# Attention weights of six chunks made in layer 0 for all queries, and a second tile set moved into the attention's pools

## Chip, cores and metric

The kernel runs on one core of one Trainium2 chip. The metric is the device time of one execution in microseconds (us). Three runs of the kernel before took 10067.42 us in the median, 10067.21 to 10070.63.

## What is computed

Two layers over 3,327 nodes of 128 features, with a dense 0/1 adjacency matrix `adj`. Cut to what matters:

```
# layer 0
h = relu(layernorm(x))
agg = adj.T @ h / deg                      # deg: row sums of adj, 0 taken as 1
x = x + relu(batchnorm(agg @ W_n.T + b_n + h @ W_c.T + b_c))
# layer 1: attention with 128 batches d, n = 3327 queries and keys, 8 features each
h = relu(layernorm(x))
q, k, v = (h @ W.T reshaped to (128, n, 8) for W in Wq, Wk, Wv)
a = softmax(q @ k.T / sqrt(128) + adj + adj, axis=keys)
x = x + (a @ v).reshape(n, 1024) @ Wo.T
```

The same `2 * adj` is added to the scores of all 128 batches. So exp(score + 2 adj) = exp(score) * exp(2 adj), and the second factor, called the weight here, can be made once.

## The kernel before

**Layer 0.** The 3,328 padded rows are 26 chunks of 128. For each chunk c, SyncE (SP) loads 128 rows of `adj` (1.66 MB) into one of three buffers `a`; TensorE (PE) adds their product with the normalised features into seven PSUM banks (`gather`, L500), ScalarE (ACT) sums the rows for the degree (L507, written to `junk`), and VectorE (DVE) takes their maximum (L510). A buffer is loaded again when all three have read it. Beside each chunk one small step of `beside` runs through the eighth bank, `aside`: a transpose and ACT's copy (L412), a product with W_c and ACT's copy (L421), or, for chunks 15 to 18, a square of a weight matrix on GpSimd (POOL, L428), a product and a maximum on DVE. From chunk 19 on, `spread` puts 1/deg into diagonal tiles on POOL (L442), PE spreads them (L446) and ACT copies (L450). After the loop come the batch norm, the second layer norm, and the projections of q, k and v for the first 416 rows, which are stored to `qT`, `kT` and `v1` in HBM (the k parts on SP's queue, the q parts on ACT's, v on POOL's). POOL's queue stores `hd` and `xd` at the end.

**Attention.** 32 groups of four batches (index i), each with 7 blocks of up to 480 queries (y) and 13 steps (s): 2,912 steps. The 26 key chunks are cut in two kinds. Of the 18 "plain" ones, DVE adds the adjacency to the scores (L923, tile `at` from `adjT`) and ACT takes the exponential (L968). For the other 8 (from chunk `WC` = 18 on), ACT takes the exponential of the scores alone (L932) and POOL multiplies by the weight (L935, tile `wt` from `wd` in HBM). PE makes the scores (L783) and the products with v (L668). Steps are written out by hand in program order, engine by engine; `fetch` issues loads of `at` and `wt` two steps ahead on SP.

**Weights.** `wd` holds 8 x 128 x 3,328 weights. Those of the first 512 queries are made after layer 0's loop, in two halves of 256 queries (`weigh_early`, L539 and L540). Those of block y + 1 are made in block y of group 0 by `more_weights`: every third step it stores the last two chunks (L804), loads two chunks (L812, 480 KB), and two steps later ACT takes their exponential (L817, tile `t`). Both use `low`, 0 or -1e30, as the bias.

**Sets.** `sets` has two sets of q, k, v tiles, one for even and one for odd groups. Both lie in a pool that is open for the whole kernel, as does `ks`, in which k is loaded before POOL sorts it (L192). `first_loads` (L877 to L892) borrows set 1's k to load the first group's k, 8 DMAs, and 16 DMAs follow for q. `loads` fetches the next set while a group runs: in group 0 from step 39 on, in later groups from step 4.

```
more_weights(i, y, s)
if x > 1:
    for args in others[:2]:
        nc.sync.dma_start(*args)
    del others[:2]
due = len(waiting) == LAG
```

Of the kernel before, what the change touches and what calls it, by code (L numbers as in the profile page):

```python
# [9 lines left out]
F32 = mybir.dt.float32  # L10
F32R = mybir.dt.float32r
I32 = mybir.dt.int32
AF = mybir.ActivationFunctionType
ALU = mybir.AluOpType
AX = mybir.AxisListType
PSUM = bass.MemoryType.PSUM
# [5 lines left out]
P = 128  # L22
NC = 26
T = N * D
NP = NC * P
NB = 512
# [4 lines left out]
SAFE = 30.0  # L31
SU = NC // 2
WC = 18
CH = 4 * NP // D
NG = D // G
DOUBLE = (3, 7, 11)
PARTS = (3, 7, 8)

# [8 lines left out]
def tile_two_layer_gnn(  # L47
# [17 lines left out]
    nc = tc.nc  # L65
# [57 lines left out]
    FROM = [3 * SU] + [LAG + 1] * (NG - 1)  # L123

    qkp = ctx.enter_context(tc.tile_pool(name="qk", bufs=1))
    ksp = ctx.enter_context(tc.tile_pool(name="ks", bufs=1))

    def tile_set(x):
        q = qkp.tile([P, NP], F32R, name=f"q{x}")
        k = qkp.tile([P, NC, P], F32R, name=f"k{x}")  # L130
        v = qkp.tile([P, G, NC, H + 1], F32, name=f"v{x}")

        nc.vector.memset(v[96:, :, NC - 1, :], 0.0)
        return q, k, v

    sets = [tile_set(x) for x in range(2)]

    def q_loads(q, p0, d, n0=0, n=NP):

# [22 lines left out]
            vd[:, (P - 1) * W :].rearrange("b (o w) -> o b w", o=1),  # L162
        )]

    def loads(tiles, d):

        q, k, v = tiles

        def dma(*args):
            return lambda: nc.sync.dma_start(*args)  # L170

        def batch(b):
            return d + b if b else d

        qs = [dma(*a) for b in range(G) for a in q_loads(q, 32 * b, batch(b))]
        vv = [dma(*a) for a in v_loads(v, d)]
        todo = []
        for half in range(2):

            ks = ksp.tile([P, NP // 2], F32R, name="ks")  # L180
            for b in range(G):
                todo += [
                    dma(*a)
                    for a in k_loads(ks, 32 * b, batch(b), half * (NP // 2), NP // 2)
                ]
            todo += vv if half == 0 else []
            todo += [qs.pop(0) for _ in range(2) if qs]
            for c in range(0, NC, 4):
                n = min(4, NC - c)

                def sort(ks=ks, c=c, n=n, half=half):
                    nc.gpsimd.tensor_copy(  # L192
                        k[:, c : c + n, half * 64 : half * 64 + 64],
                        ks.bitcast(F32).rearrange("g (p c) -> g c p", c=NC)[:, c : c + n, :],
                    )

                todo.append(sort)
                if qs:
                    todo.append(qs.pop(0))
        assert not qs  # L200
        return todo
# [105 lines left out]
    with tc.tile_pool(name="l0", bufs=1) as l0, tc.tile_pool(  # L307
        name="l0adj", bufs=3
    ) as ap, tc.tile_pool(name="l0s", bufs=4) as sp, tc.tile_pool(
        name="l0last", bufs=1  # L310
    ) as ll, tc.tile_pool(name="l0p", bufs=1, space=PSUM) as pp:


        xs = ll.tile([P, NC, D], F32, name="xs")
# [21 lines left out]
        tiles = []  # L336

        def load(c):

            a = ap.tile([P, 7 * NB], F32, name="a")  # L340
            nc.sync.dma_start(a[:, :N], adj[c * P : (c + 1) * P, :])
            tiles.append(a)
            if c in (1, 2):
                c0, c1 = (4, 14) if c == 1 else (14, NC - 1)
                nc.sync.dma_start(xs[:, c0:c1, :], xr[:, c0:c1, :])
            if c == 2:
                for p0, p1 in pieces(N - (NC - 1) * P):
                    nc.sync.dma_start(
                        xs[p0:p1, NC - 1, :], x[(NC - 1) * P + p0 : (NC - 1) * P + p1, :]
                    )  # L350
            if c in (5, 7, 9):
                i = (c - 5) // 2
                nc.sync.dma_start(wqk[i], (WqT, WkT, WvT)[i])
            if c == 11:
                nc.sync.dma_start(wo, WoT.rearrange("(e p) o -> p e o", p=P))
# [114 lines left out]
        def set_flag():  # L470
# [12 lines left out]
            nc.vector.tensor_copy(low_half, aside[:, :2])  # L483
            yield

        load(0)
        for c in range(NC):
            a = tiles[c]
            if c + 1 < NC:
                load(c + 1)  # L490
            if c < NQ:
                if c == 0:
                    stats(c)
                normalise(c, A)
                if c + 1 < NQ:
                    stats(c + 1)

            def gather(i0, i1):
                for i, (n0, w) in list(enumerate(blocks))[i0:i1]:
                    nc.tensor.matmul(  # L500
                        acc[i][:, :w], A[:, c, :], a[:, n0 : n0 + w],
                        start=(c == 0), stop=(c == NC - 1),
                    )

            last = c == NC - 1
            gather(0, 4 if last else len(blocks))
            nc.scalar.activation(  # L507
                junk, a[:, :N], AF.Copy, accum_out=deg[:, c : c + 1]
            )
            nc.vector.tensor_reduce(  # L510
                amax[:, c : c + 1], a[:, :N], AX.X, ALU.max, apply_absolute_value=True
            )
            if last:
                nc.vector.tensor_reduce(top, amax, AX.X, ALU.max)
                flags = set_flag()
                next(flags)
                gather(4, len(blocks))
                next(flags)
                spreading = spread(NQ - 1)
                next(spreading)  # L520
            if c >= 1:
                beside(c - 1)
            if c - 1 == 2 * NQ + 4:
                set_bound()

            i = c - 2 * NQ - 5
            if 0 <= i < NQ - 1 and 4 * i + 4 <= c:
                for _ in spread(i):
                    pass
        weights = []  # L530
        for n0 in range(0, NB, NB // 2):
            a = ap.tile([P, 7 * NB], F32, name="a")
            a8 = a[:, : 8 * (NB // 2)].rearrange("p (c n) -> p c n", c=8)
            nc.sync.dma_start(a8, adjr[:, WC:, n0 : n0 + NB // 2])
            weights.append((a8, n0, NB // 2))

        def weigh_early():
            a8, n0, w = weights.pop(0)
            nc.scalar.activation(a8, a8, AF.Exp, bias=low, scale=2.0)  # L539
            nc.sync.dma_start(wd[:, :, n0 : n0 + w].rearrange("c p n -> p c n"), a8)  # L540

        bst = l0.tile([P, NQ, 6], F32, name="bn_st")
        bmv = l0.tile([P, 2], F32, name="bn_mv")
# [11 lines left out]
        for i, (n0, w) in enumerate(blocks):  # L555
            s = slice(n0, n0 + w)
            nc.vector.tensor_tensor(B2[:, s], acc[i][:, :w], B2[:, s], ALU.mult)
            nc.tensor.matmul(acc[i][:, :w], wn, B2[:, s], start=True, stop=True)
            if i >= 1:
                hidden(i - 1)  # L560
            if i == 0:
                next(spreading)
            if i in (0, 1):
                weigh_early()
        hidden(NQ - 1)
        nc.vector.bn_aggr(bmv, bst.rearrange("p i s -> p (i s)"))
# [140 lines left out]
    def attention():  # L707
# [3 lines left out]
        with tc.tile_pool(name="exd", bufs=4) as ep, tc.tile_pool(  # L711
            name="adj", bufs=4
        ) as ap, tc.tile_pool(name="adw", bufs=3) as wp, tc.tile_pool(
            name="exf", bufs=6
        ) as fp, tc.tile_pool(name="res", bufs=2) as rp, tc.tile_pool(
            name="wk", bufs=2
        ) as wk, tc.tile_pool(name="psc", bufs=3, space=PSUM) as psc, tc.tile_pool(
            name="pav", bufs=1, space=PSUM
        ) as pav:


            avs2 = [pav.tile([P, NB], F32, name=f"av{x}") for x in range(2)]
            for av in avs2:
                nc.vector.memset(av, 0.0)
            if True:
# [5 lines left out]
                def at(i):  # L731
                    return i * G
# [62 lines left out]

                def more_weights(i, y, s):

                    k, phase = divmod(s, 3)
                    if i or y + 1 >= len(qblocks):
                        return  # L800
                    n0, w = qblocks[y + 1]
                    c = WC + 2 * k
                    if phase == 0 and k:
                        nc.sync.dma_start(  # L804
                            wd[c - 2 - WC : c - WC, :, n0 : n0 + w].rearrange("c p n -> p c n"),
                            have["w"][:, :, :w],
                        )
                    if c == NC:
                        return
                    if phase == 0:  # L810
                        have["w"] = wk.tile([P, 2, QB], F32, name="t4")
                        nc.sync.dma_start(  # L812
                            have["w"][:, :, :w], adjr[:, c : c + 2, n0 : n0 + w]
                        )
                    elif phase == 2:
                        a = have["w"][:, :, :w]
                        nc.scalar.activation(a, a, AF.Exp, bias=low, scale=2.0)  # L817

# [79 lines left out]
                for x, (i, y, s) in enumerate(steps):  # L900
# [1 line left out]
                    fetch(x + PRE)  # L902
                    k = x - i * SU * len(qblocks) - FROM[i]
                    if k == 0 and i + 1 < NG:
                        pending = loads(sets[(i + 1) % 2], at(i + 1))
                        total = len(pending)

                    while pending and (total - len(pending)) * (SU * len(qblocks) - FROM[i] - 4) <= k * total:
# [74 lines left out]

    def attention_shifted():

        with tc.tile_pool(name="shq", bufs=1) as shp, tc.tile_pool(
            name="adjs", bufs=2
        ) as ap, tc.tile_pool(name="exs", bufs=4) as ep, tc.tile_pool(
            name="ress", bufs=2
# [6 lines left out]
            tiles = sets[0]  # L996
            q, k, v = tiles
            with tc.For_i(0, D, G) as d0:
                for start in loads(tiles, d0):
                    start()  # L1000
                sh = shp.tile([P, N], F32, name="sh")
                for b in range(G):
# [175 lines left out]
```

## Time and profile before

| | |
|---|---|
| median of three runs | 10067.42 us (10067.21 to 10070.63) |
| profiled execution | 10069.75 us |
| its span, first to last instruction | 10068.0 us |
| mean granted TensorE clock | 0.993 |
| end of layer 0's matmuls L500 | 179 us |
| first exponential of the attention, L932 | 240.35 us |
| L932 of group 1's first step | 612.1 us |
| weight exponentials L817 | 24, median 1,097 ns |
| weight exponentials L539 | 2, 2.0 us each |

Times within the profile count from the span's start. A group's line has the line of the kernel, the engine, the operation, tile written <- tiles read, shape and count; then the sum and the mean of its durations, and how long the engine sat idle just ahead of it and what ended that. PEld is the loading of weights into TensorE, SPq the queue of SP.

### The profile page before, as it was taken

The page shows a single profiled execution, that of the slowest core. Times are in us where ns is not written, and L with a number is a line of the kernel's source. Part 1 is how long each engine was busy: PE and PEld are TensorE (multiplying, and loading weights), DVE is VectorE, ACT ScalarE, POOL GpSimd, SP SyncE. Part 2 cuts the span into 40 slices and gives each one's busy share as a digit, 9 for nine tenths or more (in the row PEclk, how much of TensorE's full clock was granted, in tenths as well). Part 3 has the DMA queues.
Part 4 walks back from the last instruction along what each step waited for, and adds up shares of the span by engine and source line. Part 5 has one row for each costly group of instructions (what it writes and reads, how often), then busy time and mean ns, then how long its engine had stood idle before and what let it go on. Part 6 is the DMA issues. An engine that isn't in the chain of part 4 may idle for free. (4 is left out here: it accounts for less than half of the span.)

```text
span 10068.0 us, 187348 instructions
## 1 busy us (share of the span) xinstructions
PE 9707.3 (96%) x71535; PEld 2723.1 (27%) x71535; DVE 9310.2 (92%) x9527; ACT 9879.0 (98%) x6662; POOL 8443.2 (84%) x4325
## 2 busy tenths in 40 slices
PE   8899999999999999999999999999999999999998
PEld 3222222222222222222222222222222222222222
DVE  6789999999999999999999999999999999999998
ACT  5899999999999999999999999999999999999998
POOL 1788888888888888888888888888888888888887
PEclk8999999999999999999999999999999999999999
DMA  7766666666666666666666666666666666666654
GB/s 259 219 184 164 168 172 175 172 167 168 167 175 173 171 168 169 167 172 172 172 170 169 167 174 171 172 168 164 172 173 172 172 164 167 172 174 172 162 157 129
DMA packets 1047069, 1735.86 MB, mean 172 GB/s; under 512 B 127342, under 2 KB 1023084, under 8 KB 1038348
## 3 DMA queue, kind: packets, MB, share of 16 engines
q1 hardware_dynamic: 1043655, 1718.90, 62.4%
q8 instruction: 562, 9.21, 0.4%
q14 instruction: 352, 2.88, 0.1%
q0 software_dynamic: 784, 4.03, 0.1%
q10 hardware_dynamic: 1716, 0.85, 0.0%
HBM read 1621.03 MB, written 102.37 MB: 171 GB/s over the span
## 5 line engine op out<-in xcount | busy, mean ns | idle before, releaser
L923 DVE SCALAR_TENSOR_TENSOR d<-at,s 128x960 f32<-128x960 f32 x8064 | 8736.8, 1140 | 475.1 <-PE s L783 328.5
L935 POOL TENSOR_TENSOR f<-f,wt 128x960 f32<-128x960 f32 (+1 forms) x3584 | 7942.2, 2235 | 1390.0 <-ACT f L932 1354.5
L968 ACT ACTIVATE d<-d 128x2880 f32<-128x2880 f32 (+1 forms) x2912 | 7072.8, 2429 | 3.9 <-DVE d L923 1.8
L668 PE MATMUL av<-d,v 128*9 128x480 f32 x32256 | 5068.5, 567 | 0.6 <-ACT d L968 0.6
L783 PE MATMUL s<-q,k 32*128 32x480 f32 x23296 | 4245.5, 476 | 311.7 <-ACT f L932 205.8
L932 ACT ACTIVATE f<-s 128x960 f32<-128x960 f32 (+1 forms) x3584 | 3446.8, 988 | 41.6 <-PE s L783 32.4
L783 PEld LDWEIGHTS s<-q,k 32*128 32x128 f32 x23296 | 1805.6, 182 | 5578.1 <-DVE d L923 3468.7
L668 PE MATMUL av<-f,v 128*9 128x480 f32 x14336 | 2851.9, 566 | 0.0
L668 PEld LDWEIGHTS av<-d,v 128*9 128x9 f32 x32256 | 583.3, 88 | 1210.2 <-issue 1208.3
L668 PEld LDWEIGHTS av<-f,v 128*9 128x9 f32 x14336 | 316.8, 88 | 154.0 <-issue 140.8
L192 POOL CAST k<-ks 128x256 fp32r<-128x256 f32 x434 | 284.0, 654 | 0.0
L239 POOL TENSOR_TENSOR o<-pf,o 104x512 fp32r<-104x512 f32 x124 | 160.0, 1290 | 9.9
L500 PE MATMUL acc<-a,A 128*128 128x512 f32 (+1 forms) x364 | 152.8, 572 | 9.1 <-DMA a<-in_adj 9.1
L678 DVE STREAM_TRANSPOSE avs<-av 128x480 f32<-128x480 f32 (+1 forms) x224 | 150.7, 673 | 4.4 <-PE av L668 4.4
L510 DVE TENSOR_REDUCE amax<-a 128x1 f32<-128x3327 f32 x26 | 93.7, 3604 | 29.7 <-DMA a<-in_adj 29.7
L442 POOL TENSOR_SCALAR o<-ident,rdeg 128x128 f32<-128x128 f32 x26 | 15.3, 604 | 111.7 <-DVE rdeg L439 111.7
L500 PEld LDWEIGHTS acc<-a,A 128*128 128x128 f32 x364 | 69.4, 194 | 95.6 <-issue 94.3
L507 ACT ACTIVATE junk<-a 128x3327 bf16<-128x3327 f32 x26 | 77.3, 2974 | 6.7 <-DMA a<-in_adj 6.7
L237 DVE TENSOR_SCALAR pf<-av,low_half 104x512 f32<-104x512 f32 x62 | 46.6, 751 | 38.7 <-PE av L208 37.5
L235 DVE COPY pf<-av 104x512 f32<-104x512 f32 x62 | 42.9, 692 | 40.6 <-PE av L208 40.6
L214 DVE COPY ov<-av 104x512 f32<-104x512 f32 x62 | 42.9, 692 | 36.0 <-PE av L208 36.0
L238 POOL CAST o<-pf 104x512 fp32r<-104x512 f32 x124 | 76.1, 613 | 0.0
(131 smaller groups left out, 901.6 us busy)
## 6 DMA issues: line engine op xcount, KB each, us to landing
at<-in_adjT SPq DMA_DIRECT2D x1728, 480.0 KB
wt<-wd SPq DMA_DIRECT2D x1536, 240.0 KB
at<-in_adjT SPq DMA_DIRECT2D x288, 448.0 KB
wt<-wd SPq DMA_DIRECT2D x256, 224.0 KB
ks<-kT SPq DMA_DIRECT2D x496, 104.0 KB
q<-qT SPq DMA_DIRECT2D x496, 104.0 KB
a<-in_adj SPq DMA_DIRECT2D x26, 1663.5 KB
kT<-o SPq DMA_DIRECT2D x128, 208.0 KB
```

The source lines that it names most:

```text
L192: nc.gpsimd.tensor_copy(k[:, c : c + n, half * 64 : half * 64 + 64], ks.bitcast(F32).rearrange("g (p c) -> g c p", c=NC)[:, c : c + n, :],)
L239: nc.gpsimd.tensor_tensor(o[:CH, 1], f[:CH], of[:CH, 0], ALU.subtract)
L500: nc.tensor.matmul(acc[i][:, :w], A[:, c, :], a[:, n0 : n0 + w], start=(c == 0), stop=(c == NC - 1),)
L507: nc.scalar.activation(junk, a[:, :N], AF.Copy, accum_out=deg[:, c : c + 1])
L510: nc.vector.tensor_reduce(amax[:, c : c + 1], a[:, :N], AX.X, ALU.max, apply_absolute_value=True)
L668: nc.tensor.matmul(av[32 * b : 32 * b + H + 1, :w], tiles[2][:, b, c, :], e, start=first, stop=last,)
L678: nc.vector.transpose(avs[:, :J, :].rearrange("p j h -> p (j h)"), av[:, : 32 * J].rearrange("p (q j) -> p j q", j=J),)
L783: nc.tensor.matmul(p[:, x, :we], k[rs, c, :], q[rs, n0 : n0 + we], start=True, stop=True,)
L923: nc.vector.scalar_tensor_tensor(d[:, j, :, :w], have[0, i, y, c // 2][:, c % 2, :w] .unsqueeze(1).to_broadcast([P, 2, w]), SAFE / 2, p[:, ...
L932: nc.scalar.activation(f[:, :, :w], p[:, :, :w], AF.Exp, scale=2.0)
L935: nc.gpsimd.tensor_tensor(f[:, :, :w], f[:, :, :w], have[1, i, y, c][:, :w].unsqueeze(1).to_broadcast([P, 2, w]), ALU.mult,)
L968: nc.scalar.activation(flat, flat, AF.Exp, scale=2.0)
```

## The change

Six of the eight chunks' weights are made in layer 0, one chunk for all 3,328 queries at a time, in two buffers `heavy`. Tile j is loaded at chunk 7 + 3j of the aggregation, clamped by POOL at chunk 8 + 3j (the clamp takes the place of the bias, which isn't known yet), put through the exponential by ACT at chunk 9 + 3j, and stored at chunk 10 + 3j. The last two chunks stay as they were made, but in one piece: `weigh_early` once for 512 queries, and `more_weights` once for each block: load at step 1, exponential at step 8, store at step 12. To make room, set 1 of q, k, v and the pool of `ks` move into the attention's pools, so they lie where layer 0 had its tiles; `attention_shifted`, a path that this data doesn't take, gets a `ks` of its own. In a set, k is now allocated ahead of q.

```diff
+NW = 6
...
-    ksp = ctx.enter_context(tc.tile_pool(name="ks", bufs=1))
-    sets = [tile_set(x) for x in range(2)]
+    sets = [tile_set(qkp, 0)]
...
+        heavy = []
+
+        def weights_of(j, phase):
+
+            if phase == 0:
+                heavy.append(lw.tile([P, NP], F32, name="heavy"))
+                nc.sync.dma_start(heavy[j], adjr[:, WC + j, :])
+            elif phase == 1:
+                nc.gpsimd.tensor_scalar(
+                    heavy[j], heavy[j], SAFE / 2, -1e30, ALU.min, ALU.max
+                )
+            elif phase == 2:
+                nc.scalar.activation(heavy[j], heavy[j], AF.Exp, scale=2.0)
+            else:
+                nc.sync.dma_start(wd[j], heavy[j])
...
+            for j in range(NW):
+                if 0 <= c - 7 - 3 * j < 4:
+                    weights_of(j, c - 7 - 3 * j)
+
             i = c - 2 * NQ - 5
             if 0 <= i < NQ - 1 and 4 * i + 4 <= c:
                 for _ in spread(i):
                     pass
-        weights = []
-        for n0 in range(0, NB, NB // 2):
-            a = ap.tile([P, 7 * NB], F32, name="a")
-            a8 = a[:, : 8 * (NB // 2)].rearrange("p (c n) -> p c n", c=8)
-            nc.sync.dma_start(a8, adjr[:, WC:, n0 : n0 + NB // 2])
-            weights.append((a8, n0, NB // 2))
+
+        a = ap.tile([P, 7 * NB], F32, name="a")
+        a8 = a[:, : (NC - WC - NW) * NB].rearrange("p (c n) -> p c n", n=NB)
+        nc.sync.dma_start(a8, adjr[:, WC + NW :, :NB])
...
-            if i in (0, 1):
+            if i == 1:
                 weigh_early()
...
+            sets.append(tile_set(qkp1, 1))
...
-                    k, phase = divmod(s, 3)
-                    if i or y + 1 >= len(qblocks):
+                    if i or y + 1 >= len(qblocks) or s not in (1, 8, 12):
                         return
                     n0, w = qblocks[y + 1]
...
+                    if s == 1:
                         have["w"] = wk.tile([P, 2, QB], F32, name="t4")
                         nc.sync.dma_start(
-                            have["w"][:, :, :w], adjr[:, c : c + 2, n0 : n0 + w]
+                            have["w"][:, :, :w], adjr[:, WC + NW :, n0 : n0 + w]
                         )
+                    a = have["w"][:, :, :w]
+                    if s == 8:
                         nc.scalar.activation(a, a, AF.Exp, bias=low, scale=2.0)
+                    if s == 12:
+                        nc.sync.dma_start(
+                            wd[NW:, :, n0 : n0 + w].rearrange("c p n -> p c n"), a
+                        )
```

More of the change, by code (lines that the diff above doesn't have):

```diff
@@ L125, in tile_two_layer_gnn, with tile_set @@
     qkp = ctx.enter_context(tc.tile_pool(name="qk", bufs=1))
-    ksp = ctx.enter_context(tc.tile_pool(name="ks", bufs=1))
-    def tile_set(x):
+    def tile_set(qkp, x):
+        k = qkp.tile([P, NC, P], F32R, name=f"k{x}")
         q = qkp.tile([P, NP], F32R, name=f"q{x}")
-        k = qkp.tile([P, NC, P], F32R, name=f"k{x}")
         v = qkp.tile([P, G, NC, H + 1], F32, name=f"v{x}")
@@ L163, in v_loads, with loads @@
         )]
-    def loads(tiles, d):
+    def loads(tiles, d, ksp):
         q, k, v = tiles
@@ L309, in tile_two_layer_gnn @@
     ) as ap, tc.tile_pool(name="l0s", bufs=4) as sp, tc.tile_pool(
-        name="l0last", bufs=1
-    ) as ll, tc.tile_pool(name="l0p", bufs=1, space=PSUM) as pp:
+        name="l0w", bufs=2
+    ) as lw, tc.tile_pool(name="l0last", bufs=1) as ll, tc.tile_pool(name="l0p", bufs=1, space=PSUM) as pp:
         xs = ll.tile([P, NC, D], F32, name="xs")
@@ L529, in tile_two_layer_gnn @@
                     pass
-        weights = []
-        for n0 in range(0, NB, NB // 2):
-            a = ap.tile([P, 7 * NB], F32, name="a")
-            a8 = a[:, : 8 * (NB // 2)].rearrange("p (c n) -> p c n", c=8)
-            nc.sync.dma_start(a8, adjr[:, WC:, n0 : n0 + NB // 2])
-            weights.append((a8, n0, NB // 2))
+        a = ap.tile([P, 7 * NB], F32, name="a")
+        a8 = a[:, : (NC - WC - NW) * NB].rearrange("p (c n) -> p c n", n=NB)
+        nc.sync.dma_start(a8, adjr[:, WC + NW :, :NB])
         def weigh_early():
-            a8, n0, w = weights.pop(0)
             nc.scalar.activation(a8, a8, AF.Exp, bias=low, scale=2.0)
-            nc.sync.dma_start(wd[:, :, n0 : n0 + w].rearrange("c p n -> p c n"), a8)
+            nc.sync.dma_start(wd[NW:, :, :NB].rearrange("c p n -> p c n"), a8)
         bst = l0.tile([P, NQ, 6], F32, name="bn_st")
@@ L714, in attention @@
             name="exf", bufs=6
-        ) as fp, tc.tile_pool(name="res", bufs=2) as rp, tc.tile_pool(
+        ) as fp, tc.tile_pool(name="qk1", bufs=1) as qkp1, tc.tile_pool(
+            name="ks", bufs=1
+        ) as ksp, tc.tile_pool(name="res", bufs=2) as rp, tc.tile_pool(
             name="wk", bufs=2
@@ L796, in more_weights @@
                 def more_weights(i, y, s):
-                    k, phase = divmod(s, 3)
-                    if i or y + 1 >= len(qblocks):
+                    if i or y + 1 >= len(qblocks) or s not in (1, 8, 12):
                         return
                     n0, w = qblocks[y + 1]
[L802 to L810, printed above, removed]
+                    if s == 1:
                         have["w"] = wk.tile([P, 2, QB], F32, name="t4")
                         nc.sync.dma_start(
-                            have["w"][:, :, :w], adjr[:, c : c + 2, n0 : n0 + w]
+                            have["w"][:, :, :w], adjr[:, WC + NW :, n0 : n0 + w]
                         )
-                    elif phase == 2:
-                        a = have["w"][:, :, :w]
+                    a = have["w"][:, :, :w]
+                    if s == 8:
                         nc.scalar.activation(a, a, AF.Exp, bias=low, scale=2.0)
+                    if s == 12:
+                        nc.sync.dma_start(
+                            wd[NW:, :, n0 : n0 + w].rearrange("c p n -> p c n"), a
+                        )
                 extra, begun = [], []
@@ L904, in attention @@
                     if k == 0 and i + 1 < NG:
-                        pending = loads(sets[(i + 1) % 2], at(i + 1))
+                        pending = loads(sets[(i + 1) % 2], at(i + 1), ksp)
                         total = len(pending)
@@ L984, in attention_shifted @@
     def attention_shifted():
-        with tc.tile_pool(name="shq", bufs=1) as shp, tc.tile_pool(
+        with tc.tile_pool(name="shk", bufs=1) as ksp, tc.tile_pool(
+            name="shq", bufs=1
+        ) as shp, tc.tile_pool(
             name="adjs", bufs=2
@@ L998, in attention_shifted @@
             with tc.For_i(0, D, G) as d0:
-                for start in loads(tiles, d0):
+                for start in loads(tiles, d0, ksp):
                     start()
```

## Prediction

> **What bounds the kernel now.** I read the page first: the busy line and the costliest groups say which engine sets the pace. Then the windows, to see where the pace is not kept; then the waits of ScalarE in the one stretch that stands out; then layer 0, where the change puts the work.
>
> ```profile
> PE 9707.3 (96%) x71535; PEld 2723.1 (27%) x71535; DVE 9310.2 (92%) x9527; ACT 9879.0 (98%) x6662; POOL 8443.2 (84%) x4325
> ...
> L968 ACT ACTIVATE d<-d 128x2880 f32<-128x2880 f32 (+1 forms) x2912 | 7072.8, 2429 | 3.9 <-DVE d L923 1.8
> ...
> L932 ACT ACTIVATE f<-s 128x960 f32<-128x960 f32 (+1 forms) x3584 | 3446.8, 988 | 41.6 <-PE s L783 32.4
> ```
>
> ACT is busy 98% of the span, and its two groups, the exponentials of the attention, sat idle 3.9 and 41.6 us in 10 ms. So the attention runs at ACT's pace. The windows show whether that holds everywhere; ACT's timeline has 112 activations L932 to a group of four batches, and so gives the groups' bounds: 240, 612, 916. The columns are the window, its length, each engine's busy time, granted clock, DMA share, GB/s.
>
> ```profile
> 240.00:612.00 372.00, 327.77 (x2160) 81.84 (x2156) 290.31 (x288) 328.55 (x226) 268.41 (x142) 0.90 0.74 212
> 612.00:916.00 304.00, 295.63 (x2224) 81.80 (x2220) 286.04 (x291) 303.97 (x204) 263.02 (x135) 1.00 0.63 170
> ```
>
> Group 1 takes 304 us with ACT busy in all of it; the later groups are the same. Group 0 takes 372: 68 us more, with ACT idle for 43 of them and the clock at 0.90. Only group 0 makes weights. Its ACT waits:
>
> ```profile
> ACT f L932 <- PE s L783: 29.1, 19, 3.8
> ACT t L817 <- DMA t<-in_adjT: 12.6, 7, 2.9
> ACT f L932 <- issue: 8.6, 1, 8.6
> ACT d L968 <- DVE d L923: 1.2, 2, 0.7
> ```
>
> The 8.6 is the start, mostly before the first f. So the 68 us are 24 weight exponentials (L817, 1.09 us each, about 1.0 on an engine whose instructions overlap: 24), 12.6 of waiting for their loads, and about 30 of waiting for scores. Group 1 has no such wait at all.
>
> Layer 0's aggregation, by windows (DMA share and GB/s are last):
>
> ```profile
> 50.00:80.00 30.00, 30.00 (x81) 14.52 (x80) 18.97 (x7) 17.35 (x16) 2.04 (x2) 1.00 0.91 333
> 80.00:110.00 30.00, 30.00 (x77) 13.96 (x75) 14.48 (x4) 19.22 (x15) 0.00 (x0) 1.00 0.75 273
> 110.00:140.00 30.00, 27.95 (x66) 11.30 (x65) 21.72 (x20) 9.72 (x8) 2.36 (x4) 0.98 0.72 254
> 140.00:170.00 30.00, 30.00 (x73) 13.94 (x72) 19.27 (x17) 17.12 (x14) 11.74 (x20) 0.97 0.62 226
> ```
>
> PE is full: a chunk's 14 matmuls and what stands beside them take 6.44 us. But DMA is far from idle: full at about 333/0.91 = 365 GB/s until 80, then busy 0.75, 0.72, 0.62. ACT is about half used, POOL nearly free.
>
> **What the Trainium skill says.** (1) "TensorE: Matmul & The Clock Gate", Part 1: a free-running window of about 3.4 us decides, and PE that was idle in one runs at half clock until a busy one has passed. The trace agrees: after a wait of 2.05 us for POOL at 136.4, PE's timeline has
>
> ```profile
> 138.48 1.97 PE L446 MATMUL aside<-o,ones 128*128 128x512 f32 x2 [2.05 <-POOL o L442]
> 140.24 6.64 PE L500 MATMUL acc<-a,A 128*128 128x512 f32 x14
> 146.72 1.02 PE L446 MATMUL aside<-o,ones 128*128 128x512 f32 x2
> 147.57 5.74 PE L500 MATMUL acc<-a,A 128*128 128x512 f32 x14
> ```
>
> so this wait cost 0.95 + 0.90 = 1.85 us besides itself. (2) "DMA: Bandwidth & Descriptors", Queues, rings and completion order: each DMA engine takes SP's descriptors in ring order, so a load issued after a store moves after it. No row of before has a large store ahead of such a load. (3) "GPSIMD Engine Reference", 3.1: one-input bodies run near 1.03 cycles an element; an estimate from that page for 3,328 elements at 1.2 GHz is 2.9 us. The trace's one-input row is slower: a cast of 512 in 613 ns (L238), so 3,328 in 4.0. I take 4.0; the two-input row (960 in 2.24, L935) gives 7.7 as the upper end.
>
> **The change, part by part.**
>
> Attention, group 0. Eighteen of 24 weight exponentials go: 18 x 1.0 = 18. So do 18 of 24 loads and stores (480 KB each way). The six left are loaded at step 1 and used at step 8, some 23 us later, against 6 us before: the 12.6 us of load waits go. So do SP's waits for ACT ahead of the stores (24.9 us on L804 in the queue's own waits), behind which at and wt loads stood. Of the 30 us of waits for scores, I look at their place: many follow a late t within 4 to 20 us, with a half-clock window between (t at 518.9 came 2.9 us late, the clock fell at 524, scores were 2.65 and 1.65 late at 537 and 542). Those go. What stays: about 5 at the start, where PE is cold anyway, and about 10 in blocks 3 to 6, where set 1's k and q are loaded at nearly twice the pace of later groups (39 to 91 steps, not 4 to 91). So 15 of 30 go. Sum 18 + 12.6 + 15 = 46, group 0 at 326. Bounds: 31 if all waits for scores stay, 58 if nearly all go.
>
> Layer 0. Six loads and six stores of 1.70 MB: 20.4 MB, at 365 GB/s 4.7 us each, 56 in all. The unused DMA time from 80 to 170 is 7.5 + 8.4 + 11.4 = 27, and the last store (4.7) lies in the tail. So at least 56 - 27 - 5 = 24 us can't be hidden. More isn't hidden, because SP is in order: the store of tile j waits for its exponential at chunk 9 + 3j, and behind it stand the load of tile j + 1 and that of a(12 + 3j). One load alone comes 7.0 us after its buffer is free (gather ends 77.6, DVE's maximum starts on landing at 84.6), each further one in a train 4.7 later, so the three take 16.4.
> - Turns from chunk 9 to 12 and 12 to 15: ACT's copy out of `aside` stands before the exponential, so it waits for PE. Gather's end + 1.5 + exponential 3.0 (2,880 elements take 2.6) + 16.4 + gather 5.6 = 26.5, against 3 x 6.44 = 19.3: 7.2 each, and once the table of Exp, 1.28. 15.7.
> - Turns 15 to 24: ACT waits for the landing only. 3.1 (degree) + 3.0 + 16.4 = 22.5 against 19.3: 3 x 3.2 = 9.6.
> - At chunks 20 and 23 the clamp stands on POOL ahead of the four L442 (2.35) that PE waits for (0.9): 4.0 + 2.35 + 0.9 = 7.25 after the tile has landed, while a(c + 1) lands 4.7 after it: 2.5 each, 5.
> - Clock: five PE waits of 4 to 9 us, each at 1.85 or somewhat less: 7.
>
> - Elsewhere on the queues: SP issues 12 DMAs more here, at 0.33 to 0.46 us each, in a queue that mostly waits. The four squares L428, which before ran at 41 and 52, now stand behind clamps, but chunks 15 to 18 need them and their tiles have landed by then: nothing, and at most a clamp, 4.0, if one is late.
>
> Sum 37. Bounds: 24 (every byte in the free time, no clock loss) and 65 (stores as slow as the rival below has them).
>
> Tail and start. Two exponentials of 2.0 become one of 1.0 and a table load goes; ACT waited 4.7 us for bn_mv after them, so nothing. The second set's k now lies over small `o` tiles of layer 0, so the first k load waits for all four qT stores, not one: issued at 215.3, it moves to about 219. DMA was full there (share 1.02 from 215 to 230), so other transfers take the place: +1, bounds 0 and +4. The moved memset waits for a store that landed long ago, and only DVE's start stands behind it: nothing.
>
> Sum: -46 + 37 + 1 = **-8 us**. The profiled execution took 10069.75 us (span 10068.0 and 1.75 around it), 2.3 above the median of the three; it would become 10061.7, the median 10059.
>
> **Rivals.**
> - *Faster.* Group 0 falls to 304 + 6 + 7 = 317 (-55) and layer 0 costs only 26, since ring and clock lose little: -55 + 26 + 0 = -29, 10038. For it: no later group waits for scores, and the free DMA time is there. Against: SP's order leaves DMA idle while the exponential runs.
> - *Slower.* One mechanism, in layer 0: the stores to wd. The one store of this size in before, xd<-xs, needed 11.7 us from issue to landing, though beside other traffic. If each of the five stores ahead of a needed load takes that, not 6.0 (4.7 and some 1.3 to land), layer 0 pays 5 x 5.7 = 28 more: 37 + 28 + 1 - 46 = +20, 10088. It decides from a store of about 7.6 us on (5 x 1.6 = 8, where the sum turns), and by over 0.2% from 11.7.
> - *Clock stays.* Group 0 keeps all its waits for scores: -31 + 37 + 1 = +7, 10074.
> That the weights aren't made as said is no rival: the order of instructions has six tiles of 3,328 columns and six loads at the later line.
>
> **How the numbers follow.** A measurement of this kernel can tell about 0.2%, 20 us, from no change. The forecast and the third rival (together 0.49) lie within it: 10045 to 10080. Faster has 0.33, slower 0.18. I predict 10059; the range 10033 to 10090 takes in both outer rivals.
>
> **What would show it.** In the changed profile: group 0's window near 326 and no wait for t; six exponentials of 3,328 near 3.0; POOL's clamp near 4.0; PE waits of 4 to 9 us for a at chunks 12, 15, 18 and for POOL at 20 and 23; the end of the aggregation at 216, not 179. It would be wrong if wd's stores take over 8 us, if the clock in group 0 stays at 0.90, or if PE does not wait in layer 0.

## Result and the profile after

The changed kernel takes 10040.95 us in the median of 11 runs (10038.73 to 10045.89), against 10067.21 (10061.61 to 10072.33) for the kernel before in the same comparison. The ratio is 0.9975 (95% interval 0.9967 to 0.9983): 26 us, or 0.25%, faster. The forecast was 8 us, with 10038 as the faster rival.

Its profiled execution took 10040.14 us, with a span of 10038.4. Here are the busy line of its page and three of its groups, with lines of the changed kernel (L984 was L968, L948 was L932). Behind the bar stand busy time in us and mean in ns, then the idle time ahead of the group and what ended it:

```profile
PE 9683.1 (96%) x71535; PEld 2727.4 (27%) x71535; DVE 9306.6 (93%) x9527; ACT 9869.9 (98%) x6649; POOL 8455.3 (84%) x4331
...
L984 ACT ACTIVATE d<-d 128x2880 f32<-128x2880 f32 (+1 forms) x2912 | 7071.9, 2429 | 6.9 <-DVE d L939 4.8
...
L948 ACT ACTIVATE f<-s 128x960 f32<-128x960 f32 (+1 forms) x3584 | 3445.0, 988 | 18.4 <-issue 8.7
...
L495 POOL TENSOR_SCALAR heavy<-heavy 128x3328 f32<-128x3328 f32 x6 | 17.8, 2960 | 128.5 <-DMA heavy<-in_adjT 80.3
```

ACT is still busy 98%, and the two exponentials take as long as before. What shrank is the idle time ahead of L948, from 41.6 to 18.4 us, and no wait for scores heads that row any more. The clamp on POOL (L495) is the new row: 2.96 us each.

The windows of group 0 and group 1 (engines, granted clock, DMA share, GB/s), with bounds from the first L948 of each group:

```profile
268.70:590.20 321.50, 301.77 (x2160) 81.22 (x2156) 287.61 (x288) 309.48 (x209) 268.51 (x142) 0.97 0.71 190
590.20:894.00 303.80, 296.03 (x2226) 82.17 (x2222) 286.16 (x291) 303.80 (x205) 262.93 (x135) 1.00 0.63 170
```

Group 0 fell from 371.8 to 321.4 us and the clock in it rose from 0.90 to 0.97; group 1 is what it was. ACT's waits in group 0:

```profile
ACT f L948 <- issue: 8.7, 1, 8.7
ACT f L948 <- PE s L804: 5.1, 6, 1.4
ACT d L984 <- DVE d L939: 4.2, 6, 0.9
ACT f L948 <- POOL f L951: 2.5, 3, 0.8
```

The wait for t is gone, and the waits for scores went from 29.1 us to 5.1.

Layer 0 pays for it. PE's timeline, with the idle time and its releaser in brackets:

```profile
92.92 8.40 PE L517 MATMUL acc<-a,A 128*128 128x512 f32 x14 [6.58 <-DMA a<-in_adj]
...
120.43 8.29 PE L517 MATMUL acc<-a,A 128*128 128x512 f32 x14 [5.81 <-DMA a<-in_adj]
...
157.66 1.13 PE L447 MATMUL aside<-o,ones 128*128 128x512 f32 x2 [2.03 <-POOL o L443]
...
187.97 2.08 PE L447 MATMUL aside<-o,ones 128*128 128x512 f32 x2 [4.07 <-POOL o L443]
189.84 7.64 PE L517 MATMUL acc<-a,A 128*128 128x512 f32 x14
```

Chunks 12 and 15 (at 92.9 and 120.4) come late and run part of their matmuls at half clock (8.40 and 8.29 us, not 5.74). At 188 PE waits for POOL, where the diagonal tiles of chunk 23 stand behind a clamp.

By stage, from each kernel's PE and ACT timelines. The first column is the end of the aggregation's matmuls, the second goes from there to the first f, the third and fourth are distances between the first f of successive groups:

| profiled execution, us | layer 0's end | start | group 0 | mean of groups 1 to 30 |
|---|---|---|---|---|
| before | 179.2 | 61.2 | 371.8 | 304.12 |
| after | 204.0 | 64.7 | 321.4 | 303.92 |
| difference | +24.8 | +3.5 | -50.4 | -0.20 |

The three stages give -22. Groups 1 to 31 with what follows are together 7.6 us shorter, which makes the -29.6 between the two profiled executions. The medians are 26.3 apart, so 3.3 of the 29.6 come from which runs were profiled.

### The profile page after: what moved, and what is told of

Its sections match the earlier page's. It is cut to its first block, busy times and chain, and to the rows that moved or that the text cites. A ratio compares the mean times of both kernels' runs of the same rounds, so it can differ in the third digit from the quotient of the medians.

```text
span 10038.4 us, 187289 instructions
## 1 busy us (share of the span) xinstructions
PE 9683.1 (96%) x71535; PEld 2727.4 (27%) x71535; DVE 9306.6 (93%) x9527; ACT 9869.9 (98%) x6649; POOL 8455.3 (84%) x4331
## 5 line engine op out<-in xcount | busy, mean ns | idle before, releaser
L984 ACT ACTIVATE d<-d 128x2880 f32<-128x2880 f32 (+1 forms) x2912 | 7071.9, 2429 | 6.9 <-DVE d L939 4.8
L948 ACT ACTIVATE f<-s 128x960 f32<-128x960 f32 (+1 forms) x3584 | 3445.0, 988 | 18.4 <-issue 8.7
L495 POOL TENSOR_SCALAR heavy<-heavy 128x3328 f32<-128x3328 f32 x6 | 17.8, 2960 | 128.5 <-DMA heavy<-in_adjT 80.3
```

Source lines behind the costliest of these rows:

```text
L948: nc.scalar.activation(f[:, :, :w], p[:, :, :w], AF.Exp, scale=2.0)
L984: nc.scalar.activation(flat, flat, AF.Exp, scale=2.0)
```

## Experiments

The theory after the result: group 0 gains by having fewer exponentials and no late load, and layer 0 loses because SP's queue is in order, so that loads wait behind a store that waits for ACT. The rivals: layer 0 loses because the bytes don't fit into its DMA time; the gain comes in part from where set 1 lies now; group 0 could have been had without layer 0.

### Sets only

Before, with set 1 and `ks` in the attention's pools and k ahead of q, no weights moved:

```diff
-    sets = [tile_set(x) for x in range(2)]
+    sets = [tile_set(qkp, 0)]
...
+            name="exf", bufs=6
+        ) as fp, tc.tile_pool(name="qk1", bufs=1) as qkp1, tc.tile_pool(
+            name="ks", bufs=1
...
+            sets.append(tile_set(qkp1, 1))
```

> The kernel before with the tile sets moved alone: set 1 of q, k, v and ks in the attention's pools, k ahead of q; the weights are made as before. Theory: the move costs what the start lost (the changed kernel takes 64.7 us from the end of layer 0's matmuls to the first exponential, before 61.2): first exponential 2 to 4 us later than before, group 0 at 372, groups 1 to 31 as before at 304.1 each, 10067 + 3 = 10070. Rival: the new places of the tiles make the later groups 0.2 us shorter each, 6 us in all (303.9 as in the changed kernel): then 10064.

Measured: 10079.94 us against 10067.02, ratio 1.0013 (1.0007 to 1.002). The start went from 61.2 to 76.6 us, where I had expected 2 to 4 us more. SP's waits from 200 to 260 begin with a line that neither before nor after has:

```profile
SPq L879 <- DMA xd<-xs: 25.5, 1, 25.5
```

Here set 1's k lies over layer 0's `xs`, whose last reader is the store to `xd`; in the changed kernel the two `heavy` tiles shift that layout, and k lies over small `o` tiles and a `heavy` tile. So a moved tile costs what its new place's last reader costs: 15 us of start here. How much of the 3.5 us in the changed kernel comes from this is tested below. Group 0 was 379.4 in this profiled execution, 7.6 longer; that execution took 10090.50, 10.6 over its median, so its parts overstate the loss. Groups 1 to 30 took 304.04 us in the mean, nearer to 304.12 than to 303.92: the move of the sets didn't make the later groups shorter, and that rival falls.

### Loads ahead

Before, all 24 exponentials kept, but each pair's load issued four steps ahead of its exponential and its store one step after. The loads stay at the steps where they were; the exponentials and stores come two steps later:

```diff
+                        for what, late_by in (("load", 0), ("exp", 4), ("store", 5)):
+                            g = yy * SU + 3 * kk + late_by
+                            pairs_at.setdefault(g, []).append((what, yy, kk))
```

> The kernel before with all 24 weight exponentials, and as many bytes, in group 0, but each load issued four steps ahead of its exponential (some 14 us) instead of two, and its store one step after that. Theory: a good part of the 68 us that group 0 took over a later one was the late loads and what they led to (12.6 us of waits, half clock, waits for scores), not the exponentials; group 0 falls to 304 + 24 + 11 = 339, layer 0 is untouched, total about 10034, a little under the changed kernel. Rival: bytes and exponentials themselves make the waits (ACT behind, PE idle, half clock): only the 12.6 go, group 0 at 359, total 10055.

Measured: 10036.48 us (10033.99 to 10042.39), ratio 0.9971 (0.996 to 0.9983); group 0 in 341.7, its clock 0.94. ACT's waits from 236 to 620:

```profile
ACT f L935 <- PE s L783: 14.2, 9, 2.8
ACT f L935 <- issue: 8.8, 1, 8.8
ACT d L971 <- DVE d L926: 1.1, 2, 0.9
```

No wait for t is left (12.6 before), and the waits for scores halved from 29.1 without one exponential being taken away. So 30 of the 68 us in group 0 came from the timing of these steps alone: 12.6 directly and some 17 more, most of it the 14.9 us of waits for scores that went with them. This kernel is as fast as the changed one, and touches nothing in layer 0.

### No weight exponentials

Before, without L817; the weights of blocks 1 to 6 are the raw adjacency:

```diff
-                        a = have["w"][:, :, :w]
-                        nc.scalar.activation(a, a, AF.Exp, bias=low, scale=2.0)
+                        pass
```

> The kernel before without the 24 exponentials L817 (the raw adjacency is stored as weight for queries from 512 on); loads, stores and their order on SP stay. Theory: the exponentials and the waits for their loads stood on ACT, so all 68 us but some 15 go: group 0 near 319. Rival: the 480 KB loads and stores and SP's waits behind them hold up at and wt: then waits for scores stay near 29 us and group 0 is at 304 + 30 = 334 or more.

Measured in a single run: 10009.14 us, group 0 in 322.4, with 12.5 us of waits for scores. The loads, the stores and their order on SP are all still there, though a store now waits only for its load; they alone don't hold group 0. The 68 us can now be split, from one profiled execution of each kernel: 371.8 - 341.7 = 30.1 for the late loads and what they led to, 341.7 - 322.4 = 19.3 for 24 exponentials (an estimate of 0.80 each, as the two kernels differ in the steps too), and 322.4 - 304.0 = 18.4 that stay without any weight exponential. Of these, 8.9 are the start. Part of the rest may still come from the weights' transfers: the changed kernel, with a quarter of them, has 5.1 us of waits for scores, not 12.5.

### Stores on POOL's queue

After, with the stores to `wd` issued by POOL:

```diff
-                nc.sync.dma_start(wd[j], heavy[j])
+                nc.gpsimd.dma_start(wd[j], heavy[j])
```

> The changed kernel with the six stores of weights issued from POOL's queue at the same chunk instead of SP's. Same bytes, same exponentials; SP no longer waits for an exponential ahead of the next load. Theory: the 25 us that the end of layer 0's matmuls moved come from SP's order (it waited 73 us for exponentials there, and DMA stood idle meanwhile), so the two waits of PE for a (6.6 and 5.8, and half clock after them) go and the end moves from 204 to 185 to 190; total 10041 - 15 = 10026. Rival: it is the bytes (20.4 MB); PE then waits elsewhere, the end stays within 4 us of 204, total within 5 of 10041.

Measured: 10026.17 us (10021.74 to 10030.49), ratio to before 0.996 (0.9947 to 0.9974). Layer 0's matmuls end at 182.7, not 204.0. PE's timeline:

```profile
86.93 5.85 PE L517 MATMUL acc<-a,A 128*128 128x512 f32 x14 [0.93 <-DMA a<-in_adj]
...
108.68 5.85 PE L517 MATMUL acc<-a,A 128*128 128x512 f32 x14 [2.59 <-DMA a<-in_adj]
```

The two waits of 6.58 and 5.81 are 0.93 and 2.59, no chunk runs at half clock after them, and the wait at chunk 23 is gone. The same bytes cost layer 0 3.5 us instead of 24.8. The median fell by 14.8 us against the changed kernel's; the profiled execution, the fastest of the five, by 18.4.

### Stores one chunk later

After, the stores still on SP's queue, but two chunks after the exponential instead of one; the last one after the loop:

```diff
-                if 0 <= c - 7 - 3 * j < 4:
+                if 0 <= c - 7 - 3 * j < 3:
                     weights_of(j, c - 7 - 3 * j)
+                elif c - 7 - 3 * j == 4:
+                    weights_of(j, 3)
```

> The changed kernel with each store of weights issued one chunk later on SP's own queue, so two chunks after its exponential and behind the load of a that it stood ahead of. Theory (SP's order, not a second ring): SP finds the exponential done, PE's waits at chunks 12 and 15 go as with POOL's queue, the end of layer 0's matmuls comes near 183 to 187, total near 10026. Rival (POOL's queue helped because its transfers take turns with SP's, while in one ring a store must hold up the loads behind it): the end stays at 195 or later, total 10034 or more.

Measured: 10019.26 us (10014.3 to 10021.29), ratio 0.9953 (0.994 to 0.9967); the end at 181.6. PE's waits for a at chunks 12 and 15 are gone; 0.67 and 0.68 us are left at 13 and 16. So it was the order in SP's queue, not the want of a second queue. The changed kernel from 80 to 85, 85 to 90 and so on to 105 shows the blocked queue (DMA share and GB/s last):

```profile
80.00:85.00 5.00, 5.00 (x13) 2.21 (x12) 0.00 (x0) 4.96 (x5) 0.00 (x0) 1.00 0.97 338
85.00:90.00 5.00, 1.33 (x5) 0.45 (x3) 0.00 (x0) 0.69 (x1) 1.05 (x1) 1.00 1.01 429
90.00:95.00 5.00, 2.08 (x3) 1.05 (x4) 2.11 (x1) 2.05 (x1) 1.91 (x1) 0.63 1.00 429
...
100.00:105.00 5.00, 5.00 (x14) 2.33 (x13) 3.49 (x2) 2.79 (x2) 0.00 (x0) 1.00 0.02 8
```

While PE stands still (1.33 and 2.08 us busy of 5) the DMA engines work off the pile of store and loads; a moment later they move 8 GB/s. SP waits for the exponential then, with the loads behind it. Its waits in the first 300 us begin:

```profile
SPq L501 <- ACT heavy L499: 73.3, 6, 19.9
```

With the later stores this wait is 23.6 us, and the windows are even and full:

```profile
60.00:80.00 20.00, 20.00 (x51) 9.41 (x50) 11.77 (x5) 13.97 (x10) 2.96 (x1) 1.00 1.02 411
80.00:100.00 20.00, 19.33 (x49) 8.95 (x48) 10.34 (x3) 14.93 (x13) 2.96 (x1) 1.00 1.01 423
100.00:120.00 20.00, 19.32 (x49) 8.26 (x48) 8.70 (x5) 15.74 (x11) 5.99 (x4) 1.00 1.01 427
```

### Order of the attention's pools

The kernel with stores on POOL's queue, and set 1's pool moved from its place behind `exf` to stand right after `exd`, so that set 1 lies over the buffers `a`:

```diff
         with tc.tile_pool(name="exd", bufs=4) as ep, tc.tile_pool(
+            name="qk1", bufs=1
+        ) as qkp1, tc.tile_pool(name="exf", bufs=6) as fp, tc.tile_pool(
             name="adj", bufs=4
```

> The kernel with the stores on POOL's queue, and the attention's pools in another order: set 1 of q, k, v over layer 0's buffers a, which are free after the aggregation, not over the small o tiles whose stores to qT come last. Theory: the 3.5 us that the start lost are the first load of k waiting for all stores to qT; they go, the first exponential comes 61 us after layer 0's last matmul instead of 65, total near 10022, faster than both kernels. Rival: DMA is full there and sets the start by its bytes: still 64 to 65, total as with POOL's stores, 10026.

Measured: 10023.05 us (10017.26 to 10026.52), ratio 0.9957 (0.9943 to 0.9971). The start is 62.6, against 65.2 with stores on POOL's queue alone. SP's waits from 200 to 270 still hold

```profile
SPq L892 <- DMA qT<-o: 5.4, 3, 3.9
```

where the changed kernel has 7.8 and before 5.6. Before had set 1 in a pool of its own, so these 5.4 us are no wait for the new place; what they are for is left open, as the k loads read `kT` and not `qT`. The start is 2.6 us shorter by the placement, in one profiled execution of each; the next experiment repeats the comparison with later stores, 64.8 to 62.7. In the total, 3 us are within the spread of runs.

### Both: later stores and the new order

> Both repairs together: stores one chunk later on SP's queue, and set 1 over layer 0's buffers a. Theory: they act in different places and add up: layer 0's matmuls end near 182, the first exponential 62 to 63 us later, total near 10017, the fastest version. Rival: the earlier start meets DMA that is full anyway, and the gain of the order is within the spread of runs: 10019 to 10022.

The edit is that of the two kernels above together. Measured: 10014.4 us (10013.81 to 10021.72), ratio to before 0.9948 (0.9935 to 0.9962). Layer 0's matmuls end at 182.6, and the start is 62.7. It is the fastest of all: 54 us below the before of its comparison (10068.44), 27 below the changed kernel. Its lead over later stores alone is within the spread.

### Loads twice

The kernel with later stores, and four of the six tiles loaded a second time into the same place, from POOL's queue, 6.8 MB more:

```diff
                 nc.sync.dma_start(heavy[j], adjr[:, WC + j, :])
+                if j < 4:
+                    nc.gpsimd.dma_start(heavy[j], adjr[:, WC + j, :])
```

> The kernel with the stores one chunk later, with four of the six tiles loaded twice, the second time from POOL's queue into the same tile before the clamp: 6.8 MB more between 48 and 130 us, nothing else. Theory: DMA at its full rate of some 428 GB/s (2.14 MB in 5 us, as measured in the changed kernel) had free time left, so the end of layer 0's matmuls moves by less than the 16 us that four loads of 1.70 MB take: 2 to 8 us. Rival (the prediction's reckoning at 365 GB/s, by which the free time was used up already): it moves by 16 us or more.

Measured in a single run: 10038.18 us; layer 0's end at 198.1, 16.5 later than with later stores. My theory, that free DMA time was left over, falls. The rival's number came true, but not the rate in it: the queue moved 427 GB/s, not 365. Four loads of 1.70 MB at 425 GB/s are 16.0 us. The window that shows it best, 80 to 100:

```profile
80.00:100.00 20.00, 13.84 (x34) 6.00 (x32) 5.29 (x2) 10.63 (x9) 2.20 (x2) 0.91 1.01 427
```

GB/s is what it was in the kernel with later stores; PE has 13.84 us of work in it instead of 19.33. One thing besides bytes changed: the clamps wait for the second load, and ACT waited 22.2 us for them ahead of the exponential. PE's longest wait was still for a (6.34 us of 8.1 in all; with later stores all of them are 1.9); 3.91 and 2.35 us were for POOL's squares behind clamps. How the 16.5 us divide between bytes and order isn't settled by one run, so its nearness to 16.0 proves nothing. That no room was left from 80 to 140 us is shown by the share of 1.01 there in both kernels; from 160 to 180 it is 0.80 with later stores.

## Why the prediction was right and wrong

**The direction was right and the mechanism in the main; the size was not.** The forecast's sum was -46 + 37 + 1 = -8; the profile has -50.4 + 24.8 + 3.5 = -22. The prediction itself called 20 us its smallest difference from no change, so that -8 had the right sign says little. What happened is near the faster rival's sum, -55 + 26 + 0, but that is in part luck: the rival had layer 0 at 26 because ring and clock lose little, and the 24.8 are ring, clamp and clock.

**Group 0, -46 against -50.4.** The load waits went as said. Eighteen exponentials were worth some 18 x 0.80 = 14.5, not 18, by the difference of the two experiments. The mis-sized term is the waits for scores: I let 15 of 30 stay, 10 of them in blocks 3 to 6 from the loads of set 1. In fact 5.1 of 29.1 stayed, and the two errors partly cancel. The chain read from the trace (a late t, a half-clock window, late scores) was sized rightly: in the loads-ahead run 14.9 us went and 14.2 stayed, 10.7 of them in blocks 3 to 6. The step that failed is the reason for those 10. In the changed kernel set 1 is still loaded in these blocks, and its waits for scores there are 1.7 us; without exponentials but with all transfers of weights they are 6.1. So most of them hung on the weights' exponentials and transfers, not on the loads of set 1; which of the two it was is open. The 5.1 is partly chance: with later stores, where group 0's program is the same, 10.0 stayed, 4.8 of them in these blocks. The rival in which group 0 keeps its clock fell: 0.97.

**Layer 0, +37 against +24.8.** Term by term:
- Turns 9 to 15: predicted 15.7, measured 6.58 + 5.81 = 12.4, at the chunks named and for the reason named. The train of three transfers, taken as 16.4 us at 365 GB/s, took 14.4 and 14.6 from the store's issue to the landing of a.
- Turns 15 to 24: predicted 9.6, measured nothing: PE has no wait for a at chunk 18, 21 or 24. Two steps failed. The train was again shorter: from the store's issue at 126.4 to the landing of a at 141.1 it took 14.7, and 15.3 and 14.5 in the next two turns. And PE's own pace was taken as 3 x 6.44 = 19.3, but a chunk with a square beside it takes 6.73 (before, chunks 16 and 17 begin at 110.40 and 117.13), and after the wait at chunk 15 came half clock. From chunk 15 to 18 PE took 143.1 - 120.4 = 22.6, so that even the predicted 22.5 would have left it no wait. At chunk 24 the tile did come late, at 186.4, when chunk 23 had ended at 183.9; PE's wait for POOL hid it. The window from 126 to 141 shows the rate of the first of these three:

```profile
126.00:141.00 15.00, 15.00 (x37) 6.08 (x36) 8.41 (x4) 6.43 (x5) 3.72 (x2) 1.00 1.00 406
```

- Behind clamps: predicted 5 for chunks 20 and 23; measured 0 and 4.07. The clamp was 2.96, not 4.0. My estimate from the Trainium skill ("GPSIMD Engine Reference", 3.1) was 2.9, and I took the row of a cast instead: a different operation on another shape was the worse guide.
- Clock: predicted 7 for five waits; measured 2.66 and 2.55 after the two waits for a, 1.06 + 1.90 after the one for POOL, less the 1.74 that before lost at its own wait and after didn't: 6.4. And chunk 8's matmuls came 1.3 us later, which I hadn't counted.

12.4 + 4.07 + 6.4 + 1.3 = 24.2 of the 24.8.

**The floor of 24 was wrong in itself**, and that the result lies next to it is luck: moving only the store brought layer 0's cost to 3.5 and 2.4. I had divided 333 GB/s by a busy share of 0.91 and called 365 GB/s full; with a full queue the transfers ran at 423 to 429. Nor is one less the share free time: in before's steady stretch a load came every 6.44 us at a share of 0.75, so it counted as 4.8 us, and in a full queue it takes 1.70 MB / 425 GB/s = 4.0. Reckoned anew from the windows of before with 425, as an estimate made after the result: 30 x (152 + 171 + 199) for 80 to 170 and 20 x 97 for 60 to 80, where before moved 314 and later stores 411, is about 17.6 MB of room, against 18.7 MB for six loads and five stores. That leaves 1.1 MB or 2.6 us over, near the 2.4 measured with later stores. The Trainium skill ("DMA: Bandwidth & Descriptors", Bandwidth) gives 425 for a 16 MB load on a single core, which these windows agree with. Its limit of about 358 for HBM to SBUF, under "Where 436 GB/s comes from", is passed by them; under Bandwidth the page ties that figure to two cores that stream at once, and here one core ran.

**The start, +1 against +3.5**, within its bounds. I had taken full DMA queues to cover the later k loads. Counted from layer 0's end, k was loaded 2.6 us later (38.7 instead of 36.1), and that reached the first f, as the new pool order shows by taking 2.6 and 2.1 away in its two comparisons.

**The slower rival** needed stores of over 7.6 us. It fell: from the store's issue at 78.5, three transfers had landed by 92.9, 14.4 us for all, and no later train took over 15.3.

**Open:** the 7.6 us in groups 1 to 31. The move of the sets doesn't explain them (304.04 in the mean with it alone), and loads ahead without moved sets have 303.93 as well. The spread of before alone is 10.7 us over 11 runs, so this may be no effect at all.

## What to carry to other kernels

In a queue that is in order, put a store that waits for compute behind the loads that the next stage needs, or on another engine's queue: here that was worth 22 and 15 us, beside the 26 that the change had gained. Before moving work away from a stage that stalls, ask how much of the stall is lateness: two more steps between a load and its use gained as much as moving three quarters of the work. And take a full queue's rate from a window in which the queue is full, not from a rate divided by a busy share.

## Unexpected on the hardware

- Transfers of 1.70 MB (the loads called 1.66 MB above, in units of 1,024) ran at 423 to 429 GB/s while the queue was full. In the changed kernel 338 GB/s were moved from 80 to 85 us, just after a store of that size had been issued at 78.5, and 429 in the 10 us after.
- A PE wait of 2.0 us was followed by half clock in before (1.97 and 6.64 us for what takes 1.02 and 5.74) and not in after (1.13, then 5.74). The Trainium skill ("TensorE: Matmul & The Clock Gate", Part 1) has half clock follow an idle window of some 3.4 us that runs freely. The traces agree on the windows: the granted clock changes only at times that lie 3.41 us, or a multiple of it, apart. They don't agree that PE must be idle in all of one, as the prediction had read them. In before the wait, 136.43 to 138.48, lies wholly within one window, in which PE was busy for 1.37 us, and half clock was granted in the next (granted clock, DMA share and GB/s are last):

```profile
135.20:138.62 3.42, 1.37 (x5) 0.53 (x4) 3.32 (x6) 0.00 (x0) 2.36 (x4) 1.00 0.49 117
138.62:142.03 3.41, 3.41 (x5) 1.35 (x6) 3.34 (x5) 1.54 (x2) 2.00 (x4) 0.50 0.93 394
```

In after, windows counted on from the clock's change at 125.39 have a boundary at 156.11, inside the wait of 155.63 to 157.66. The same wait in four other kernels fits: it lies within one window with later stores and with the new order, and half clock follows; a boundary cuts it with stores on POOL's queue and in the kernel with both changes, and none follows.
